# Convolution, Fourier mixer and FP8 feed-forward on one core: last stores, first loads and pixel loads moved, down's weights widened to 128 columns

## The chip, the cores and the metric

The kernel runs on one core of one Trainium2 chip. The metric is device time in microseconds of one execution; a kernel's figure is the median of several runs. A profiled execution is a run of its own, with its own time.

## What is computed

Input x has shape 64 x 55 x 55 x 96 (batch, rows, columns, channels). The first layer is a depthwise convolution with a 25 x 25 kernel of which only every third row and column is kept, and not the centre:

```python
lat = depthwise_conv(x, raw_kernel * mask, padding='SAME')
x = lat * x + bias + x
```

Then each image is a sequence of 3025 tokens of 96 channels:

```python
t = x as (64, 3025, 96)
h = relu(bn1(layernorm(t) @ w1.T))             # 192 channels
X = fft(h, over the tokens, 'ortho')
y = ifft(relu(affine(X.real, X.imag)) + 1j * relu(affine'(X.real, X.imag))).real
t = t + bn2(y @ w2.T)
t = t + ffn(layernorm(t))                      # 96 -> 384 -> 96
```

The feed-forward part rounds its operands to an 8-bit float (5 exponent, 2 mantissa bits) and its sums to a 16-bit one.

## The kernel before, in words

**Build and constants.** SyncE (SP) loads the 81 taps of each channel (`kt`) and a table of selectors (`sel`, 3.9 MB, four DMAs, line 92). ScalarE's queue loads the small parameters, and VectorE works out the constants from them. Then (lines 199 to 215) TensorE multiplies selectors with taps and so makes banded matrices, in 56 PSUM tiles `pt`; ScalarE copies the bands of the first 48 channels to `toep`, VectorE those of the other 48 to `later`, one copy each for a tile. Six DMAs (line 217) store `later` to the DRAM scratch `tb`, 8.4 MB in all.

**Convolution** (lines 222 to 327). Work goes in 12 groups: a half of the channels (48), a residue r of the row number modulo 3, a half of the batch (bh, 32 images). A group has 4 tiles of rows for r = 0 and 3 for r = 1 and r = 2, and 6 steps of 8 channels. `load` fetches the pixels `x` of one step, a tile of 384 KB by one DMA on SP, two steps ahead of use; the first two steps' loads are issued after the build. `compute` does one tile in one step: two PSUM tiles `pl` of 4 channels each, matmuls of `toep` with the pixels of the tile and its neighbours (line 253), one VectorE product (line 261) into the output buffer `buf`, one GpSimd addition of the bias (line 271). There are 8 PSUM tiles and 6 output buffers (`ob`, `NOB`). `stores` makes the list of DMAs that bring a finished buffer to the DRAM scratch `t1`: large ones of 288 KB on ScalarE's queue (line 292) and small ones of 54 or 18 KB on GpSimd's; in the last group every second large one is on SP. They are issued over the following group's steps (line 326), or at once (`early`, line 315) where the next group's tiles need the buffers; in the last group all are issued at once. During the sixth group (`halfway`) `toep` is loaded again from `tb` (line 317).

**Main stage.** After the convolution, `m1` and `m2` (0.8 and 1.0 MB) are loaded on ScalarE's queue. Each of the 64 sequences has 289 tasks on the five engines. Its `t` (121 partitions of 25 tokens, 1.16 MB) is loaded by SP (line 549; 5 buffers), VectorE takes statistics (line 560, 25 instructions), GpSimd, ScalarE and VectorE make the layer norm's factor (`variance`, `root`, `inverse`, `newton`), GpSimd scales it to `xa`, and TensorE does:

- `turn` (pa, line 587), `hidden` (ph, 609), `dft_j` (pf, 624). The result `g` (3 buffers) is put to DRAM by SP in seven puts (line 644), and fetched in another layout as `gt` (line 664);
- `dft_r` (px, line 692, the first that needs `m1` and a fetch), `project` (pd, 767 and 777), `inverse_k1` (pe, 797), back through DRAM again, `inverse_k2` (py, 859);
- the feed-forward part: `turn` (pq, 913), `up` (pu, 936), `down` (pw, 981). `down` has 75 matmuls a sequence, each with 121 token columns of the FP8 activations `hq` as weights and 96 columns of `w2q` moving. `up` has 128 columns of `w1q` as weights and up to 512 moving.

The order of all tasks is worked out when the program is built: every task has an engine, a cost and a place, and `ordered` plays the engines forward, taking tasks by place when their inputs and buffers are free. The tasks are then issued in that order, so each engine's order is fixed.

Of the kernel before, what the change touches and what calls it, by code (L numbers as in the profile page):

```python
# [50 lines left out]


@with_exitstack
def conv_attn_hybrid(ctx, tc, a, out, t1, tb, gds, eds):
# [9 lines left out]
    def const(name, shape, src=None, dt=F32, pool=None):  # L64
        x = (pool or cst).tile(shape, dt, tag=name, name=name)
        if src is not None:
            nc.scalar.dma_start(x, src)
        return x
# [4 lines left out]

    order = tc.manual_schedule()
    order.__enter__()
    with ExitStack() as cx:
        ccst = cx.enter_context(tc.tile_pool(name="c_cst", bufs=1))
        toep = ccst.tile([128, CHH, NE * TQ], F32, tag="toep", name="toep")
        cbias = ccst.tile([128, CH], F32, tag="cbias", name="cbias")
        ps = cx.enter_context(tc.tile_pool(name="c_ps", bufs=8, space=PSUM))  # L80
        xp = cx.enter_context(tc.tile_pool(name="c_x", bufs=2))
        first = cx.enter_context(ExitStack())
        selp = first.enter_context(tc.tile_pool(name="c_sel", bufs=1))
        pp = first.enter_context(tc.tile_pool(name="prep", bufs=1))
        lp = first.enter_context(tc.tile_pool(name="c_later", bufs=1))
        later = lp.tile([128, CHH, NE * TQ], F32, tag="later", name="later")
        kt = selp.tile([128, CH], F32, tag="kt", name="kt")
        nc.sync.dma_start(kt, a["taps"])
        sel = selp.tile([128, TQ, SU * TQ], F32, tag="sel", name="sel")
        for j0 in range(0, TQ, 5):  # L90
            j1 = min(j0 + 5, TQ)
            nc.sync.dma_start(sel[:, j0:j1], a["sel"][:, j0:j1])


        bns = {k: pp.tile([128, 4, w], F32, tag=f"bn{k}", name=f"bn{k}") for k, w in ((1, H), (2, CH))}
        rest = pp.tile([1, 2 * CH], F32, tag="rest", name="rest")
        vecs = [bns[1][:, :2].rearrange("p n w -> p (n w)"), bns[1][:, 2:].rearrange("p n w -> p (n w)")]
        vecs += [bns[2].rearrange("p n w -> p (n w)"), rest]
        for n, of in enumerate(vecs):
            n0, n1 = 4 * CH * n, min(4 * CH * (n + 1), 4 * (H + CH) + 2 * CH)  # L100
            nc.scalar.dma_start(of[:1], a["vec"][:, n0:n1])
        par = const("par", [128, 2, 6], a["par"])
        w1t = pp.tile([CH, H], F32, tag="w1t", name="w1t")
        nc.scalar.dma_start(w1t, a["w1t"])
        w2t = pp.tile([128, 2, CH], F32, tag="w2t", name="w2t")
        nc.scalar.dma_start(w2t, a["w2t"])
        fw1 = pp.tile([CH, FF], F32, tag="fw1", name="fw1")
        nc.scalar.dma_start(fw1, a["fw1t"])
        fw2 = pp.tile([128, 3, CH], F32, tag="fw2", name="fw2")
        nc.scalar.dma_start(fw2, a["fw2t"].rearrange("(k p) c -> p k c", p=128))  # L110
        fb1 = pp.tile([128, 3], F32, tag="fb1", name="fb1")
        nc.scalar.dma_start(fb1, a["fb1"])
        f1 = const("f1", [NJ, 4 * KHP], a["f1"])
        i2 = const("i2", [4 * KHP, NJ], a["i2"])
        ident = const("ident", [128, 128])
        ident8 = const("ident8", [NJ, NJ], dt=F8)
        w1e = const("w1e", [97, H])
        w2e = const("w2e", [128, 2, CH])
        w1q = const("w1q", [CH, FF], dt=F8)
        w2q = const("w2q", [128, 3, CH], dt=F8)  # L120
        b1q = const("b1q", [128, 3])
        b2q = const("b2q", [NJ, CH], dt=F16)
        nrd = const("nrd", [128, 2, 1])
        eps = const("eps", [NJ, 1])

        tnts = [const(f"tnt{k}", [97, 4 * NJ]) for k in range(2)]
        nc.vector.memset(eps, 1e-5)
        one = pp.tile([1, 128], F32, tag="one", name="one")
        nc.vector.memset(one, 1.0)
        ones = pp.tile([CH, CH], F32, tag="ones", name="ones")  # L130
        nc.vector.memset(ones, 1.0 / CH)
        zero = pp.tile([3 * NR1, CH], F32, tag="zero", name="zero")
        nc.vector.memset(zero, 0.0)
        for of in (toep, later):
            nc.gpsimd.memset(of[:, :, : 2 * TQ], 0.0)
            nc.gpsimd.memset(of[:, :, 16 * TQ :], 0.0)
        make_identity(nc, ident)
        for k in range(2):
            nc.gpsimd.memset(tnts[k][96:97, :], 1.0)

        for n, of in enumerate(vecs):
            width = 4 * CH if n < 3 else 2 * CH
            pv = ps.tile([128, 512], F32, tag="ps", name=f"pv_{n}")
            nc.tensor.matmul(pv[:, :width], one, of[:1], start=True, stop=True)
            if n < 3:
                nc.vector.tensor_copy(of, pv[:, :width])
        nc.vector.tensor_copy(cbias, pv[:, :CH])
        fb2q = pp.tile([NJ, CH], F8, tag="fb2q", name="fb2q")
        nc.vector.tensor_copy(fb2q, pv[:NJ, CH : 2 * CH], saturate=False)
        nc.vector.tensor_copy(b2q, fb2q)  # L150


        nc.vector.tensor_scalar(par[:, :, 4:5], par[:, :, 3:4], -1.0, None, ALU.mult)
        nc.vector.tensor_scalar(par[:, :, 5:6], par[:, :, 1:2], -1.0, None, ALU.mult)
        nc.vector.tensor_scalar(nrd, par[:, :, 0:1], -1.0, None, ALU.mult)
        bias2 = pp.tile([NR1, CH], F32, tag="bias2", name="bias2")
        for k, width in ((1, H), (2, CH)):
            bn = bns[k]
            v, r, q = (pp.tile([128, width], F32, tag=f"{x}{k}", name=f"{x}{k}") for x in ("v", "sc", "sq"))
            nc.vector.tensor_scalar(v, bn[:, 3, :], 1e-5, None, ALU.add)  # L160

            nc.scalar.activation(q, v, AF.Sqrt)
            nc.vector.reciprocal(r, q)
            nc.vector.tensor_tensor(q, r, r, ALU.mult)
            nc.vector.tensor_tensor(q, q, v, ALU.mult)
            nc.vector.tensor_scalar(q, q, -0.5, 1.5, ALU.mult, ALU.add)
            nc.vector.tensor_tensor(r, r, q, ALU.mult)
            nc.vector.tensor_tensor(r, r, bn[:, 0, :], ALU.mult)
            row, of = (w1e[96:97, :], slice(96, 97)) if k == 1 else (bias2, slice(0, NR1))
            nc.vector.tensor_tensor(row, bn[of, 2, :], r[of, :], ALU.mult)  # L170
            nc.vector.tensor_tensor(row, bn[of, 1, :], row, ALU.subtract)
            if k == 1:

                nc.vector.tensor_tensor(w1t, w1t, r[:96, :], ALU.mult)
                pm = ps.tile([128, 512], F32, tag="ps", name="pm")
                nc.tensor.matmul(pm[:CH, :H], ones, w1t, start=True, stop=True)
                nc.vector.tensor_tensor(w1e[:96, :], w1t, pm[:CH, :H], ALU.subtract)
            else:
                for h in range(2):
                    nc.vector.tensor_tensor(w2e[:, h, :], w2t[:, h, :], r, ALU.mult)  # L180

        for ed in eds:
            pad = ed.rearrange("r q k c -> q r k c")[:, :, KH, :]
            nc.sync.dma_start(pad[0], bias2)
            for q in range(1, 4):
                nc.sync.dma_start(pad[q], zero[NR1 * (q - 1) : NR1 * q])
        nc.vector.tensor_copy(w1q, fw1, saturate=False)
        nc.vector.tensor_copy(w2q, fw2, saturate=False)
        fb1q = pp.tile([128, 3], F8, tag="fb1q", name="fb1q")
        nc.vector.tensor_copy(fb1q, fb1, saturate=False)  # L190
        nc.vector.tensor_copy(b1q, fb1q)
        nc.vector.tensor_copy(ident8, ident[:NJ, :NJ], saturate=False)

        for j0 in range(0, TQ, 5):
            nj = min(5, TQ - j0)
            for e in range(2, 16):  # L200
                pt = ps.tile([128, 512], F32, tag="ps", name=f"pt_{e}_{j0}")
                for jj in range(nj):
                    for p in range(2):
                        u0 = (15 - e + 3 * p) * TQ
                        nc.tensor.matmul(
                            pt[64 * p : 64 * p + 64, jj * CH : (jj + 1) * CH],
                            sel[:, j0 + jj, u0 : u0 + 64],
                            kt,
# [807 lines left out]
    for b in range(B):  # L1016
        sequence(b)
# [127 lines left out]
```

## Time and profile before

| | us |
|---|---|
| median of 3 runs | 4634.52 (4630.35 to 4637.94) |
| the profiled execution | 4654.67 |
| its span, first to last instruction | 4652.9 |
| busy: TensorE matmuls | 4284.9 |
| busy: VectorE | 3280.7 |
| busy: ScalarE | 2963.2 |
| busy: GpSimd | 3087.5 |
| last matmul of the build ends | 61.35 |
| convolution's first matmul of the chain | 86.57 |
| convolution's last matmul ends | 950.4 |
| main stage's first matmul | 1021.7 |

A slice row divides the span into 40 equal parts; each digit is the busy share of a part in tenths. PEclk is the clock granted to TensorE, in tenths. The chain of waits goes back from the last instruction, at each step to what released it; a piece has its start, its length, and what it was. In the groups of instructions a name such as `hq` is a tile, and 128x121 is partitions by elements. PE is TensorE, PEld its weight loads, DVE VectorE, ACT ScalarE, POOL GpSimd, SP SyncE; a q after an engine is its queue. A fp32 matmul has two records.

### The profile page before, as it was taken

The numbers are of one execution on the slowest core, as the hardware profiler recorded it, in microseconds if no ns is written. First come the engines' busy times: TensorE is split into PE (matmuls) and PEld (weight loads), VectorE is DVE, ScalarE is ACT, GpSimd is POOL, SyncE is SP. The second block draws the span as 40 slices with busy tenths as digits, with TensorE's granted clock in tenths as the row PEclk, the third lists the DMA queues.
The fourth block names the chain that finished last, engine by engine and source line by source line (L and its number), as shares of the span: only waits on it lengthen the run. The fifth ranks groups of instructions, "written<-read, shape, count | busy, mean of one in ns | idle before, by whom it ended". The sixth has DMA issues, their size and how long they took to land.

```text
span 4652.9 us, 194788 instructions
## 1 busy us (share of the span) xinstructions
PE 4284.9 (92%) x83314; PEld 3569.2 (77%) x83314; DVE 3280.7 (71%) x7232; ACT 2963.2 (64%) x5947; POOL 3087.5 (66%) x4209
## 2 busy tenths in 40 slices
PE   7998798939999999999999999999999999999987
PEld 6998798937777777777777777777777777777775
DVE  4544354424888877877887788788787878788776
ACT  2000000017888888887887888888887888788875
POOL 1766576745666767766776666677766666677655
PEclk8999899969999999999999999999999999999996
DMA  4678888786666666766676666676666666667662
GB/s 162 166 193 204 245 197 207 190 185 165 165 171 178 179 177 178 181 177 169 180 183 169 169 174 179 172 185 180 176 183 169 177 174 176 171 179 183 177 162 71
DMA packets 572798, 823.14 MB, mean 177 GB/s; under 512 B 62127, under 2 KB 470276, under 8 KB 570268
## 3 DMA queue, kind: packets, MB, share of 16 engines
q1 hardware_dynamic: 442704, 736.10, 58.7%
q10 hardware_dynamic: 113036, 64.71, 7.1%
q0 software_dynamic: 16192, 9.86, 1.1%
q8 instruction: 655, 10.73, 1.0%
q14 instruction: 211, 1.73, 0.1%
HBM read 419.45 MB, written 390.64 MB: 174 GB/s over the span
## 4 chain that ended last, share of the span: by engine, by line
PE 71%; DVE 7%; DMA 7%; ACT 6%; issue 5%; POOL 2%; ACTq 2%; SPq 0%; POOLq 0%; DVEq 0%
PE pl L253 13%; PE pf L624 9%; PE ph L609 9%; PE pd L767 7%; PE px L692 7%; PE pw L981 5%; PE py L859 4%; PE pd L777 4%; PE pu L936 4%; PE pe L797 3%; PE pa L587 3%; DMA x<-in_xc_dram 2%; DMA t<-buf 2%; DVE y L945 2%; PE pq L913 2%
## 5 line engine op out<-in xcount | busy, mean ns | idle before, releaser
L253 PE MATMUL pl<-x,toep 128*64 128x96 f32 (+1 forms) x18432 | 790.1, 250 | 99.0 <-DVE buf L261 41.2
L253 PEld LDWEIGHTS pl<-x,toep 128*64 128x64 f32 (+1 forms) x18432 | 783.4, 137 | 105.7 <-issue 55.7
L945 DVE CAST y<-pu 128x1008 f16<-128x1008 f32 (+1 forms) x576 | 689.2, 1202 | 224.6 <-PE pu L936 220.5
L261 DVE SCALAR_TENSOR_TENSOR buf<-pl,x 121x384 f32<-121x384 f32 (+1 forms) x480 | 390.1, 842 | 499.0 <-PE pl L253 314.3
L609 PEld LDWEIGHTS ph<-w1e,tnt 97*121 97x121 f32 x3200 | 543.3, 185 | 210.9 <-issue 64.4
L960 ACT ACTIVATE hq<-z 128x1008 fp8e5<-128x1008 f16 (+1 forms) x576 | 601.2, 1050 | 156.7 <-DVE z L948 156.3
L718 DVE SCALAR_TENSOR_TENSOR m<-px,par,m 128x400 f32<-128x400 f32 x768 | 480.8, 626 | 286.3 <-ACT ar L709 201.6
L609 PE MATMUL ph<-w1e,tnt 97*121 97x192 f32 x3200 | 665.1, 330 | 12.9 <-ACT e L806 11.4
L271 POOL TENSOR_TENSOR buf<-buf,cbias 121x768 f32<-121x768 f32 (+1 forms) x240 | 434.1, 1821 | 363.9 <-DVE buf L261 252.1
L624 PE MATMUL pf<-h,f 121*128 121x384 f32 (+1 forms) x1664 | 664.8, 484 | 4.9 <-ACT h L618 2.6
L521 ACT ACTIVATE sm_s_a<-sm_v_a,eps 121x25 f32<-121x25 f32 x64 | 20.3, 318 | 959.0 <-POOL sm_v_a L512 956.6
L574 POOL TENSOR_TENSOR xa<-t,rstda 121x384 f32<-121x384 f32 (+1 forms) x448 | 348.2, 780 | 419.7 <-PE pa L587 411.7
L692 PE MATMUL px<-m,gt 50*64 50x50 f32 x24576 | 456.4, 220 | 63.1 <-issue 59.8
L692 PEld LDWEIGHTS px<-m,gt 50*64 50x64 f32 x24576 | 416.0, 136 | 122.0 <-issue 105.2
L725 POOL TENSOR_TENSOR sm<-ar,m 128x400 f32<-128x400 f32 x256 | 270.9, 1058 | 353.6 <-DVE m L718 296.4
L767 PE MATMUL pd<-w2e,sm 128*64 128x96 f32 x8192 | 415.7, 254 | 30.9 <-ACT g L628 18.0
L628 ACT COPY g<-pf 128x384 f32<-128x384 f32 (+1 forms) x832 | 385.6, 467 | 85.5 <-PE pf L624 70.6
L1001 POOL TENSOR_TENSOR ot<-t,o 121x480 f32<-121x480 f32 x320 | 374.3, 1177 | 91.2 <-DVE o L995 91.2
L618 ACT ACTIVATE h<-ph 121x384 f32<-121x384 f32 (+1 forms) x832 | 389.8, 488 | 68.3 <-PE ph L609 61.6
L948 DVE TENSOR_SCALAR z<-y,b1q 128x1008 f16<-128x1008 f16 (+1 forms) x576 | 418.9, 732 | 11.4
L767 PEld LDWEIGHTS pd<-w2e,sm 128*64 128x64 f32 x8192 | 358.6, 139 | 76.0 <-ACT g L628 22.5
L981 PEld LDWEIGHTS <-hq 128*121 128x121 fp8e5 x4800 | 315.9, 142 | 77.1 <-issue 37.6
(115 smaller groups left out, 8367.2 us busy)
## 6 DMA issues: line engine op xcount, KB each, us to landing
gd<-g SPq DMA_DIRECT2D x768, 192.0 KB
gt<-gd SPq DMA_DIRECT2D x512, 288.0 KB
x<-in_xc_dram SPq DMA_DIRECT2D x240, 384.0 KB
t<-t SPq DMA_DIRECT2D x64, 1050.0 KB
out_dram<-ot SPq DMA_DIRECT2D x320, 210.0 KB
t<-buf ACTq DMA_DIRECT2D x211, 288.0 KB
ed<-e SPq DMA_DIRECT2D x384, 150.0 KB
ed<-e SPq DMA_DIRECT2D x128, 131.2 KB
```

Source lines behind the costliest of these rows:

```text
L253: nc.tensor.matmul(pl[p : p + width, cc * NBS : (cc + 1) * NBS], toep[:, c0 + g + cc, o : o + width], xts[n, c0, m + d][:, g + cc, :], sta ...
L261: nc.vector.scalar_tensor_tensor(buf[:px, :, c0 + g : c0 + g + CG].rearrange("p n c -> p c n"), pl[:px, : CG * NBS].rearrange("p (c n) -> ...
L271: nc.gpsimd.tensor_tensor(part, part, cbias[:px, c1 : c1 + CC].unsqueeze(1).to_broadcast([px, NBS, CC]), ALU.add)
L609: nc.tensor.matmul(x[:NJ, q * H : (q + 1) * H], live[tnt][:, g * NJ : (g + 1) * NJ], w1e, start=True, stop=True,)
L624: nc.tensor.matmul(x[:, : nq * H], f1, live[h][:, : nq * H], start=True, stop=True)
L692: nc.tensor.matmul(x[to : to + 64].rearrange("p (q r n) -> p q r n", q=2, r=2)[:, k2p, :, o : o + NR1], y[rows, k % KC, c0 : c0 + 64], m1[ ...
L718: nc.vector.scalar_tensor_tensor(live[out_], view(px)[:, :, 256 : 256 + KC * NR1], scale, live[than], ALU.mult, ALU.max)
L767: nc.tensor.matmul(y[k % 2][64 * k2p : 64 * k2p + 64, k // 2 * CH : (k // 2 + 1) * CH], full[:, k, 64 * k2p : 64 * k2p + 64], w2e[:, 0, :] ...
L945: nc.vector.tensor_copy(live[y16][:, :n], live[pu][:, :n])
L948: nc.vector.tensor_scalar(make(z16, "z16", [128, 1024], F16)[:, :n], live[y16][:, :n], b1q[:, k : k + 1], 0.0, ALU.add, ALU.max,)
L960: nc.scalar.activation(live[hq][:, k, n0 : n0 + n], live[z16][:, :n], AF.Copy, saturate=False)
L981: nc.tensor.matmul(p[:NJ, g * CH : (g + 1) * CH], live[hq][:, k, n0 : n0 + NJ], w2q[:, k, :], start=(k == 0), stop=(k == 2),)
```

## The change

1. The pixel loads of the first two steps stand ahead of `kt` and `sel` on SP. The first two residues of each batch half change places, so that the first group has 3 tiles.
2. The other half's bands lie in three tiles, of 14, 14 and 20 channels: VectorE makes three copies for each PSUM tile, and three DMAs store them. The first two lie in a new tile `shared`.
3. Two of the six output buffers lie in `shared` as well, later four of the five `t` buffers; three others lie at the far end of the memory (`obs`) and outlive the convolution.
4. `t1` is two tensors, one for each half of the batch. Load, statistics and layer norm of sequences 0 and 1 (the first 10 tasks of each) are issued within the convolution's last two steps and behind it.
5. The last group's 36 stores are issued in the main stage, one with every third task of the order, all on SP. `m1` and `m2` are loaded on SP ahead of them.
6. `hq` has 7 more columns, zeroed once; `down` takes 128 of them as weights and writes 128 rows, of which 121 are used.
7. The zeroing of parts of `tnt`, `sm`, `sr` and `hq` is issued at their first use in the main stage. The tasks' places stand in a table (the former formulas' values, rounded to five digits). Costs and buffer counts of the planner stay.

```diff
+    def made_ahead(k):
+
+        return k // len(PLACES) < AHEAD and k % len(PLACES) < NAHEAD
+
...
+        place = k // len(PLACES) + PLACES[k % len(PLACES)]
...
+        if pool == "t":
+            if k % 5 == 4:
+                live[h] = sb("t", shape, f"t_{k}", bufs=1)
+                return live[h]
+            o = tw * (k % 5)
+            live[h] = shared[:NJ, o : o + tw].rearrange("p (h g c) -> p h g c", h=2, c=CHH)
...
-            tv = t1[b].rearrange("h (j r) c -> j h r c", r=NR1)
+            tv = t1s[b // BB][b % BB].rearrange("h (j r) c -> j h r c", r=NR1)
...
-                            p[:NJ, g * CH : (g + 1) * CH],
-                            live[hq][:, k, n0 : n0 + NJ],
+                            p[:, g * CH : (g + 1) * CH],
+                            live[hq][:, k, n0 : n0 + 128],
...
+    shared = const("shared", [128, 4 * tw])
...
-        later = lp.tile([128, CHH, NE * TQ], F32, tag="later", name="later")
+        bounds = (0, 14, 28, CHH)
+        later = [
+            shared[:, 14 * k * NE * TQ : 14 * (k + 1) * NE * TQ].rearrange("p (c n) -> p c n", n=NE * TQ)
+            for k in range(2)
+        ]
+        later.append(lp.tile([128, CHH - 28, NE * TQ], F32, tag="later2", name="later2"))
...
-        groups = [(0, r, bh) for r, bh in ((0, 0), (1, 0), (0, 1), (1, 1), (2, 0), (2, 1))]
+        groups = [(0, r, bh) for r, bh in ((1, 0), (0, 0), (1, 1), (0, 1), (2, 0), (2, 1))]
...
+        for step in steps[:2]:
+            load(*step)
+        kt = selp.tile([128, CH], F32, tag="kt", name="kt")
...
-                nc.vector.tensor_copy(later[:, :, cols], src[:, CHH:])
-        for c0 in range(0, CHH, CC):
-            nc.sync.dma_start(tb[:, c0 : c0 + CC], later[:, c0 : c0 + CC])
+                for k, of in enumerate(later):
+                    nc.vector.tensor_copy(of[:, :, cols], src[:, CHH + bounds[k] : CHH + bounds[k + 1]])
+        for k, of in enumerate(later):
+            nc.sync.dma_start(tb[:, bounds[k] : bounds[k + 1]], of)
...
-        ob = cx.enter_context(tc.tile_pool(name="c_ob", bufs=NOB))
+        ob = cx.enter_context(tc.tile_pool(name="c_ob", bufs=1))
+        obs = obx.enter_context(tc.tile_pool(name="c_obs", bufs=3, side="right"))
...
+                turn_ = (sum(NTS[r] for _, r, _ in groups[:n]) + m) % NOB
+                if turn_ < 4:
+                    pool = obs if turn_ else ob
+                    bufs_[n, m] = pool.tile([128, NBS, CHH], F32, tag="buf", name=f"buf_{n}_{m}")
+                else:
+                    o = 2 * tw * (turn_ - 4)
+                    bufs_[n, m] = shared[:, o : o + NBS * CHH].rearrange("p (n c) -> p n c", c=CHH)
...
+                if n == len(groups) - 1 and ending:
+                    for k_ in ahead[:3]:
+                        tasks[k_][3]()
+                    ahead = ahead[3:]
+                if m < early and n + 1 < len(groups):
...
+            if n == len(groups) - 1 and c0 == 3 * CC:
+                for b in range(AHEAD):
+                    tasks[len(PLACES) * b][3]()
...
-        for queue, to, of in pending:
-            queue.dma_start(to, of)
+        for k in ahead:
+            tasks[k][3]()
...
-    m1 = const("m1", [128, KHP, 2 * NR1], a["m1"], pool=late)
-    m2 = const("m2", [128, KHP, 64], a["m2"], pool=late)
+    m1 = const("m1", [128, KHP, 2 * NR1], a["m1"], pool=late, queue=nc.sync)
+    m2 = const("m2", [128, KHP, 64], a["m2"], pool=late, queue=nc.sync)
...
-        for k in ordered(bufs):
-            tasks[k][3]()
+        for n, k in enumerate(in_order):
+            if not made_ahead(k):
+                tasks[k][3]()
+            if n % 3 == 0 and pending:
+
+                to, of = pending.pop(0)[1:]
+                nc.sync.dma_start(to, of)
+                if not pending:
+                    obx.close()
```

## The prediction

> **What bounds the kernel now.** I read the page's busy times and its 40 slices first, then the busy times of chosen stretches, then the chain of waits where TensorE stands still, and last the PEld groups.
>
> ```profile
> PE   7998798939999999999999999999999999999987
> PEclk8999899969999999999999999999999999999996
> DMA  4678888786666666766676666676666666667662
> ```
>
> One slice is 116 us. TensorE is full but for the first slice, slice 9 (930 to 1047 us) and the end. The stretches (us, busy time of each engine, then clock, DMA share, GB/s):
>
> ```profile
> 16.00:62.00 46.00, 45.35 (x1065) 45.16 (x1064) 25.86 (x73) 21.73 (x57) 0.00 (x0) 1.00 0.02 5
> 66.00:82.00 16.00, 0.00 (x0) 0.00 (x0) 0.00 (x0) 0.00 (x0) 0.00 (x0) 0.51 1.02 422
> 955.00:990.00 35.00, 0.00 (x0) 0.00 (x0) 0.00 (x0) 0.00 (x0) 10.94 (x18) 0.50 0.82 159
> 990.00:1020.00 30.00, 0.00 (x0) 0.00 (x0) 7.31 (x46) 0.63 (x2) 1.55 (x7) 0.50 1.01 240
> 1500.00:4500.00 3000.00, 2870.31 (x53888) 2288.54 (x53885) 2406.76 (x5586) 2472.79 (x4960) 2099.59 (x3122) 0.99 0.68 176
> ```
>
> Two stretches have an idle TensorE and a saturated DMA: after the build (8.4 MB of the second half's table go out, pixels behind them), and from the convolution's last matmul (950.4) on. The last row is the main stage: 53,888 matmul records at 997 a sequence (83,314 less 19,506 of build and convolution, over 64) are 54.1 sequences, 55.5 us each, ScalarE busy 45.7, VectorE 44.5. The chain at the seam (start, length, what):
>
> ```profile
> 965.29 12.46 DMA t<-buf
> 977.76 12.12 DMA t<-buf
> ...
> 989.96 13.86 DMA t<-t
> ...
> 1003.90 4.10 DVE sta L560 x25
> ...
> 1009.45 10.08 issue
> ...
> 1021.70 1.85 PE pa L587 x8
> ...
> 1053.67 1.12 PE px L692 x64
> ...
> 1072.18 0.92 PE px L692 x64
> ```
>
> Last stores, first load, its statistics, then TensorE; 32 us later px, the first task that needs data written to DRAM and fetched back.
>
> **The build.** From 61.35 to 86.57 TensorE waits: 25.2 us. The pixels of two steps now stand ahead of the selectors: 6 x 0.39 = 2.36 MB, 7 us at the 339 GB/s of 5 to 10 us, so the first selectors land at some 13 us; the build starts at 15.95, behind VectorE's constants (0 to 4 us late). VectorE's copy of 240 elements (0.41 us alone, 0.34 back to back) becomes three, 0.53 us together by a fixed 0.09 us each; TensorE takes 0.82 us a group, so this hides (uncovered 56 x 0.2 = 11 us; at the end 0.2 us shows). Convolution can start at 62, but the 8.4 MB still flow until 62.2 + 19.9 (422 GB/s) + 1.5 = 83.6. By the tile sizes one of the first group's output buffers lies where the third part of the table was: VectorE waits for that part's store. TensorE runs on through 8 PSUM tiles: a step is 224 matmul records at 42.3 ns (the chain's 82.69 us for 1954) = 9.5 us, 8 tiles are step 0 and a third of step 1, 12.2 us; it stops at 74, resumes at 84.5 and ends step 1 at 91. Step 2's pixels wait for space that VectorE frees late, and land at 92. Before, those 19 us of work end at 107.5 (86.57 + 19, and 1.9 for the clock of 0.50 up to 90). Gain 15.5; without the buffer wait step 2's pixels still queue behind the table, gain 21; with late selectors and the buffer, 10. Less than nothing is excluded: the pixels now land before the build ends. I take 15.
>
> **The seam.** Two loads of t (2.3 MB) go under the last group; t1 is split by batch, so they wait only for stores long done. They stand on SP behind the last pixel load, with nothing but m1, m2 after them. Their 50 statistics (4.1 us a sequence by the row x25) go on VectorE, behind which wait the products that free PSUM tiles; VectorE is busy half of that stretch and 8 tiles are some 11 us of TensorE work, so I count 0 (5 if t comes late). The ScalarE root stands behind the sixth group's stores on ScalarE's queue, which before ended at 961. So the main stage's first matmul moves from 1021.7 to about 960. That isn't the gain: what is late next is DMA. SP now holds, in this order, m1 and m2 (1.87 MB), three loads of t (3.48 MB), and the 36 last stores (18 x 288 KB and 18 small: 6.08 MB), one at every third task, 19 of them ahead of the first put of g and all ahead of the first fetch; then the puts (2.46 MB) and one fetch (0.61 MB). With three g buffers TensorE stops after some 12 us until that put. Stores at 150 GB/s (146 from 950 to 980, 159 from 955 to 990): 40.5 us; the other 8.4 MB at 240: 35 us; landing 3: px at 951 + 78.5 = 1029.5 instead of 1053.7, a gain of 24. From there both run the same tasks (the places are the old numbers rounded to five digits, the costs unchanged, down's too). Less 4 for the convolution's end, where 2.3 MB join a DMA at 0.78 to 0.93: I take 20. Bounds: 0, and 62 if nothing waits.
>
> All on one queue: the nine stores that SP issued took 40.9 us, 4.5 each. At that price 18 large ones take SP 82 us, and with 12 for the small ones (0.66 each on GpSimd, line 315) px comes at 951 + 35 + 3 + 12 + 82 = 1083, 29 us late. Against it stands the Trainium skill, "DMA: Bandwidth & Descriptors", section "Issuing engines are not separate DMA queues": transfers from all issuers share 16 engines, and more issuers save only issue time. The trace is nearer to the rule: while SP needed 4.5 us a store, ScalarE and GpSimd ran 27 others, and the sum was 150 GB/s at share 0.8. I keep 24.
>
> The zeroing of tnt, sm, sr and hq moves into GpSimd's main stage, 0.93 + 0.76 + 0.53 us once, where it waits for puts anyway (uncovered 2.2 us). The new group order has the same tiles, stores and early counts: 0, within 5 us either way.
>
> **down with 128 columns.** The groups of weight loads (line, names, shapes, count, busy, mean ns), then pieces of the chain:
>
> ```profile
> L981 PEld LDWEIGHTS <-hq 128*121 128x121 fp8e5 x4800 | 315.9, 142 | 77.1 <-issue 37.6 <-ACT hq L960 15.2 <-ACT d L786 1.2
> L913 PEld LDWEIGHTS <-xq 121*96 121x96 fp8e5 x1600 | 124.1, 127 | 78.2 <-POOL xq L904 31.8 <-issue 16.9 <-POOL sr L725 0.5
> L936 PEld LDWEIGHTS <-w1q 96*128 96x128 fp8e5 x1152 | 102.5, 101 | 47.3 <-issue 20.3 <-DVE nc L718 2.7
> ```
>
> ```profile
> 3024.90 0.83 PE pw L981 x15
> ...
> 3031.28 1.82 PE pw L981 x30
> ...
> 3099.77 0.21 PE pq L913 x4
> ...
> 3102.82 0.43 PE pu L936 x2
> ```
>
> Down (pw) takes 55 ns a matmul. pu streams 504 columns in 215 ns, 0.43 ns each; pq's 121 columns then need 52 and take 53: bound by its columns. pw's 96 need 41 and take 55: bound by loading 121 columns of hq. The load of 128 fp8 columns (101 ns) is shorter than that of 96 (127). So with 128 columns the 96 moving ones should bind: 42 ns, 13 saved, x 75 = 0.97 us a sequence, x 64 = 62 us of TensorE work.
> Two rules of the Trainium skill ("TensorE: Matmul & The Clock Gate") bear on it. "Weight-path perf modes — Fast Weight Load (FWL) and DoubleRow" has a fast load for exactly 128 columns that aren't fp32, as the rows say. "Wait — 56ns, not 53.3ns?" speaks against: the sequencer may spend 62 ns on each matmul, and then 55 to 60 ns is its floor and the gain 0. But the px piece runs 64 records in 0.92 us, 14 ns each. I take 13 ns; more is excluded by the 96 columns. Other end: hq's columns start at odd byte offsets (121 g), w1q's don't; if that turns the fast load off, seven more columns cost 7 x 0.6 ns (the slope of 127 to 142), 4 ns, 20 us in all.
> How much of 62 shows? pw holds 6.7% of the chain from 1500 to 4500, 3.7 of its 4.15 us a sequence: at most 0.89. But TensorE's pieces add up to 50.3 of 55.5 us and ScalarE is busy 45.7; the order was set with the old cost, so part turns into waits for ScalarE and VectorE. Between 0.3 and 0.89 I take 0.6: 37 us.
>
> **Sum.** 15 + 20 + 37 = 72 us off the profiled execution (4654.67, span 4652.9): 4583. The median, 4634.52, is 20 below that execution, so 4562.5.
>
> **Rivals.**
> - The fast load stays off (15%). For: the odd offsets; no row shows such a load. Down costs 20 x 0.6 = 12: 4634.5 - 15 - 20 + 12 = 4611.5.
> - The seam gives nothing, because bytes only change places (12%). For: DMA share 0.8 to 1.0 through it. 4634.5 - 15 - 37 = 4582.5.
> - The seam gives all, puts passing between stores (12%). For: 1030 to 1050 has share 0.62. 4634.5 - 15 - 62 - 37 = 4520.5.
> - Slower (9%): SP waits for a store's landing before it can issue the next, and every put and fetch of the main stage's start stands behind that. Place: SP from 953 on. A landing takes 9.3 us (median of the nine and their like, line 315), px then starts at 1001 + 18 x 9.3 = 1168, 115 late: 4634.5 + 115 - 15 - 37 = 4697.5. It decides from 5.8 us a large store, where px is 52 late. For it: SP's longest wait there was 12 us; against it: 4.5 us a store with three issuers.
>
> **Numbers.** The sum as worked has 52%. The range, 4515 to 4620, reaches from the whole-seam case with a little more from down to the fast-load case with a poorer seam (it ends at 4631 with none). Outside it are the slow case and edges of those two. Within 0.2% (9 us, about what a measurement of this kernel can tell from no change) only the fast-load rival with a seam of nothing ends: 3%. Slower 9%, faster 88%.
>
> **What would show it.** Convolution's first matmul near 62, with a stop near 74 to 84; main stage's first matmul near 960, a TensorE gap until a put, px near 1030; PEld of hq near 100 ns and 15 pw in 0.63 us; ScalarE's share up. Wrong if PEld of hq is over 142, if px comes after 1054, or if pw's time shrinks and the period of 55.5 doesn't.

## The result, and the profile after

| | before | after |
|---|---|---|
| median of the paired runs, us | 4636.21 (4630.35 to 4637.94, 4 runs) | 4574.73 (4566.3 to 4588.28, 4 runs) |
| ratio of after to before | | 0.9872, 95% interval 0.9846 to 0.9899 |
| the profiled execution | 4654.67 | 4572.36 |
| its span | 4652.9 | 4570.5 |
| first matmul of the convolution | 85.6 | 61.1 |
| last matmul of the convolution | 950.2 | 929.6 |
| first matmul of the main stage (pa) | 1021.7 | 940.8 |
| first px | 1053.6 | 1035.2 |
| us a sequence, from 1500 to 4500 us | 55.50 | 54.63 |

The kernel is 1.28% faster, some 60 us; 72 were predicted. The period of the last row is 3000 us times 997 records a sequence, divided by TensorE's records in the stretch. One execution's milestones scatter: after and the kernel `e1_down121` below have the same code up to px, and px comes 10 us apart. A milestone of a single profile is therefore good to some 15 us.

The 40 slices of after:

```profile
PE   8999898949999999999999999999999999999996
PEclk9999999969999999999999999999999999999996
DMA  4788888876666666766666666666666666667662
```

The first slice is fuller. Slice 9 (914 to 1028 us) is almost as empty as before, 4 where it was 3. The stretches behind the build and the main stage (columns as before):

```profile
72.00:76.00 4.00, 3.47 (x84) 3.28 (x82) 0.00 (x0) 0.00 (x0) 0.00 (x0) 1.00 1.04 441
76.00:80.00 4.00, 1.91 (x48) 1.72 (x42) 0.00 (x0) 0.00 (x0) 0.00 (x0) 1.00 1.02 428
80.00:84.00 4.00, 0.00 (x0) 0.00 (x0) 0.00 (x0) 0.00 (x0) 0.00 (x0) 0.53 0.90 317
...
1500.00:4500.00 3000.00, 2853.68 (x54752) 2244.59 (x54750) 2471.53 (x5662) 2493.30 (x5011) 2120.82 (x3158) 0.99 0.68 178
```

TensorE starts the convolution at once, fills its PSUM tiles while VectorE (third busy column) does nothing, and stops from 78 to 86 us. The chain shows what it waited for, a store of the table and then VectorE's product into the output buffer that lies where this part of the table was:

```profile
64.17 20.87 DMA tb<-later
...
85.32 0.81 DVE buf L1008
...
86.18 43.87 PE pl L1000 x1006
```

In the main stage TensorE does 864 more records in 3000 us than before, with 17 us less of busy time. The group of `down`'s weight loads, and two of its pieces in the chain:

```profile
L762 PEld LDWEIGHTS <-hq 128*128 128x128 fp8e5 x4800 | 232.6, 100 | 88.4 <-issue 46.2 <-ACT hq L742 18.6 <-ACT d L572 0.5
```

```profile
3194.90 0.64 PE pw L762 x15
...
3195.97 0.72 PE pw L762 x15
```

A load takes 100 ns where it took 142, and 15 matmuls 0.64 to 0.72 us where they took 0.83. At the seam, the chain from the convolution's end to px, and then what SP issued there:

```profile
934.95 22.14 DMA t<-buf
957.11 0.87 SPq L1100
...
1018.41 0.71 SPq L1100
1019.22 2.46 SPq L432
1021.73 2.89 DMA gd<-g
...
1024.72 0.07 ACT g L416
...
1035.30 1.12 PE px L478 x64
```

```profile
958.94 27.36 SPq L1100 DMA_DIRECT2D t<-buf  x17
986.41 3.11 SPq L432 DMA_DIRECT2D gd<-g  x2
989.56 5.96 SPq L1100 DMA_DIRECT2D t<-buf  x5
995.62 3.13 SPq L432 DMA_DIRECT2D gd<-g  x2
998.85 11.07 SPq L1100 DMA_DIRECT2D t<-buf  x7
```

From 957 on the chain is almost only SP's own queue: the last stores (L1100) stand between the puts of g (L432). ScalarE can't copy into one of the three buffers g before its put has landed; it waited 49.4 us for puts in four waits, the last until 1024.6. TensorE's work behind that copy then runs up to px. This wait has taken the place of the last stores and the first load of t.

### The profile page after: what moved, and what is told of

The parts are those of the page before. It is cut to its first block, busy times and chain, and to the rows that moved or that the text cites. A ratio compares the mean times of both kernels' runs of the same rounds, so it can differ in the third digit from the quotient of the medians.

```text
span 4570.5 us, 194901 instructions
## 1 busy us (share of the span) xinstructions
PE 4227.5 (92%) x83314; PEld 3487.6 (76%) x83314; DVE 3311.5 (72%) x7344; ACT 2953.9 (65%) x5947; POOL 3071.1 (67%) x4196
## 4 chain that ended last, share of the span: by engine, by line
PE 62%; DVE 9%; DMA 9%; ACT 8%; issue 6%; POOL 4%; SPq 2%; ACTq 1%; POOLq 0%; DVEq 0%
PE pl L1000 13%; PE pf L412 9%; PE ph L397 8%; PE px L478 6%; PE pd L553 6%; PE py L644 4%; PE pu L718 3%; PE pd L563 3%; PE pe L583 3%; PE pa L376 2%; DMA x<-in_xc_dram 2%; PE pw L762 2%; DVE y L727 2%; POOL xq L686 1%; ACT m L495 1%
## 5 line engine op out<-in xcount | busy, mean ns | idle before, releaser
L363 POOL TENSOR_TENSOR xa<-shared,rstda 121x384 f32<-121x384 f32 (+1 forms) x364 | 283.2, 781 | 366.7 <-PE pa L376 360.8
L1008 DVE SCALAR_TENSOR_TENSOR buf<-pl,x 121x384 f32<-121x384 f32 (+1 forms) x336 | 270.9, 842 | 291.8 <-PE pl L1000 176.9
L1018 POOL TENSOR_TENSOR buf<-buf,cbias 121x768 f32<-121x768 f32 (+1 forms) x168 | 303.4, 1819 | 237.2 <-DVE buf L1008 184.9
L412 PEld LDWEIGHTS pf<-h,f 121*128 121x128 f32 x1664 | 293.3, 192 | 93.0 <-ACT h L406 24.0
L782 POOL TENSOR_TENSOR ot<-shared,o 121x480 f32<-121x480 f32 x260 | 304.3, 1178 | 81.2 <-DVE o L776 81.2
```

The source lines that it names most:

```text
L412: nc.tensor.matmul(x[:, : nq * H], f1, live[h][:, : nq * H], start=True, stop=True)
L782: nc.gpsimd.tensor_tensor(halves(y), live[t][:, :, 5 * q : 5 * q + 5], halves(live[o16]), ALU.add)
```

## The experiments

Twelve kernels, each timed against the kernel before on its chip. The median of the kernel before differs from one comparison to the next (4625 to 4643 us), so kernels are compared by their ratios. The lead at 900 us is the surplus of TensorE's records over the kernel before, at the convolution's 23.6 records a us; the lead at px is 1053.6 less the time of the first px. Both are from one execution each.

| kernel | ratio | 95% interval | lead at 900 | lead at px |
|---|---|---|---|---|
| after | 0.9872 | 0.9846 to 0.9899 | 18.6 | 18.4 |
| e1_down121 | 0.9933 | 0.9907 to 0.9959 | 26.0 | 29.0 |
| e2_down128_alone | 1.0020 | 1.0002 to 1.0039 | 0.4 | 3.0 |
| t_fixed_ring | 1.0006 | 0.9983 to 1.0028 | -1.1 | 6.1 |
| x_places_and_down | 0.9866 | 0.9842 to 0.9889 | 2.1 | 23.7 |
| e5_pixels_behind_build | 0.9923 | 0.9896 to 0.9951 | 10.4 | 10.6 |
| e4_seam_undone | 0.9847 | 0.9822 to 0.9871 | 28.1 | 46.9 |
| e7_one_t1 | 0.9867 | 0.9839 to 0.9895 | 21.7 | 42.0 |
| e9_seam_undone_down121 | 0.9903 | 0.9878 to 0.9928 | 25.9 | 46.3 |
| e3_own_queues | 0.9820 | 0.9793 to 0.9847 | 23.4 | 52.7 |
| e6_stores_after_fetch | 0.9895 | 0.9866 to 0.9923 | 18.9 | 76.0 |
| q_stores_scalar_gpsimd | 0.9837 | 0.9811 to 0.9864 | 18.8 | 43.1 |
| c_own_queues_down_cost | 1.0592 | 1.0565 to 1.0618 | 25.8 | 50.2 |

A difference of two ratios has an interval of some 0.0037 to either side (the two half-widths, added as squares and the root taken), 17 us.

**e1_down121**: after, with `down` as before.

```diff
-                            p[:, g * CH : (g + 1) * CH],
-                            live[hq][:, k, n0 : n0 + 128],
+                            p[:NJ, g * CH : (g + 1) * CH],
+                            live[hq][:, k, n0 : n0 + NJ],
```

> The kernel after with down's weights back at 121 columns (all else as after). My theory: the wider weights are worth more than the 37 us of the prediction, because the main stage's period fell from 55.5 to 54.6 us a sequence, 53 us in all; the medians leave 43 for it beside 18 at the first px. So this kernel comes out 40 to 62 us over the kernel after (4575), at 4615 to 4637, its period back at 55.5 us and the PEld of hq back near 142 ns. Rival: the shorter period is from the other parts (t buffers at fixed places, layer norms made ahead); then it stays within 15 us of 4575.

Measured 4604.0 us, ratio 0.9933: 0.0061 above after, 28 us give or take 17, and less than the 40 to 62 that were expected. The weight load is back at 138 ns. So within the changed kernel `down` is worth some 0.4 of the 68 us of TensorE time that it saves, and by the interval 0.2 to 0.7.

**e2_down128_alone**: before, with only `down` changed (`hq` in a fixed tile with seven zeroed columns more).

```diff
+    hqp = late.tile([128, 3, NJ * NR1 + 7], F8, tag="hq0", name="hq0")
+    padded["hq"] = [hqp]
...
-                            live[hq][:, k, n0 : n0 + NJ],
+                            live[hq][:, k, n0 : n0 + 128],
```

> The kernel before with 128 weight columns in down alone. If the wider weights work by themselves, this is 40 to 60 us under the kernel before (4636), at 4576 to 4596, with the PEld of hq near 100 ns and conv and seam as before (first px near 1054). If they need the rest of the change, less than 25 us.

Measured 4652.88 us, ratio 1.0020 with an interval of 1.0002 to 1.0039: 9 us lost, give or take 9. The weight load takes 99 ns here too, so the saving is there, and no time comes of it:

```profile
1500.00:4500.00 3000.00, 2830.30 (x53483) 2227.37 (x53482) 2422.39 (x5578) 2461.39 (x4940) 2092.16 (x3117) 0.99 0.69 176
```

TensorE was busy 40 us less than before in these 3000 us, and did 405 records fewer: it waited more. This miss led to x and t.

**e5_pixels_behind_build**: after, with the first pixel loads behind the table's stores again.

```diff
-        for step in steps[:2]:
-            load(*step)
...
             nc.sync.dma_start(tb[:, bounds[k] : bounds[k + 1]], of)
         first.close()
+        for step in steps[:2]:
+            load(*step)
```

> The kernel after with the first pixel loads behind the table's stores, as before. The prediction had 15 us for this step, the trace has the convolution's end 24 us earlier: 4590 to 4599. First matmul of the convolution near 86 again. If the convolution's later stalls absorb the early start, within 6 us of the kernel after.

Measured 4608.81 us, ratio 0.9923: 24 us above after, give or take 18. The convolution starts at 85.5 us again. At 150 us its lead, counted in the same way, is -0.4 us, where the nine kernels with pixels ahead have 9.6 to 15.6, 12.7 in the mean; at 900 us it is 10.4, where they have 18.6 to 28.1, 23.0 in the mean. Both put the pixels at some 13 us.

**e4_seam_undone**: after, with no task made ahead, the last stores issued at once on their three queues, and `m1`, `m2` on ScalarE's. t and its buffers keep their new places.

```diff
-AHEAD, NAHEAD = 2, 10
+AHEAD, NAHEAD = 0, 10
...
-                if m < early and n + 1 < len(groups):
+                if m < early:
...
         order.__exit__(None, None, None)
+    obx.close()
```

> The kernel after with the seam as before: no task made ahead, last stores issued at once on three queues, m1 and m2 on ScalarE's queue. My theory now: the seam's part of the change gave nothing (from the convolution's last matmul to the first px it is 109 us after and 103 before), so this is within 10 us of the kernel after, with first px at 1025 to 1040. The prediction's 20 us would make it 4595; a gain hidden elsewhere in the trace would too.

Measured 4568.89 us, ratio 0.9847: 0.0025 below after, which the intervals don't part from zero. px came 89 us after the convolution's last matmul, in after 106, before 103. So the spreading itself gained nothing. Undoing it did not undo the seam, though: the loads of t still moved forward, for SP issued them from 917 us on, ahead of the last stores. They go to `shared`, where no buffer of the last group lies, and wait only for the stores of the group ahead of it.

**e7_one_t1**: e4, with t1 one tensor as before.

```diff
-            t1s = [dp.tile([BB, 2, NTOK, CHH], F32, tag=f"t1_{k}", name=f"t1_{k}") for k in range(BH)]
+            t1 = dp.tile([B, 2, NTOK, CHH], F32, tag="t1", name="t1")
+            t1s = [t1[BB * k : BB * (k + 1)] for k in range(BH)]
```

> The kernel with the seam undone (tasks not made ahead, stores at once) and t1 one tensor again, as in before. From the convolution's last matmul to the first px the seam-undone kernel took 90 us and before 103; if that comes of the split (sequence 0's load no longer waits for the last stores), this one is back at 101 to 105, and 12 us slower than the seam-undone kernel (ratio near 0.987). If dependencies are kept by region anyway, within 5 us of it (ratio 0.9847).

Measured 4559.37 us, ratio 0.9867, and px 83 us behind the convolution's end: with the seam undone the split of t1 gives nothing that shows.

**e9_seam_undone_down121**: e4 with e1's edit.

> The kernel with the seam undone and down back at 121 columns. Down's wider weights gave 28 us (e1 against after) in the kernel after and nothing (9 us slower) in the kernel before. If they pay in every kernel with the other parts, this one is 25 to 40 us over the seam-undone kernel, ratio 0.990 to 0.993. If what they pay depends on the seam (tasks ahead, stores spread), the difference is under 10 us, ratio under 0.987.

Measured 4579.75 us, ratio 0.9903: 0.0056 above e4, 26 us give or take 16, and 0.0036 above e7. That repeats e1. It also says that the rest of the change (places, group order, pixels, and the small parts with them), without `down` and without the spreading, is worth 45 us.

**x_places_and_down**: e4 with the pixels behind the build and the old group order; of the change the places of the buffers and tiles, the three-part table, the split of t1 and `down` are left.

> The seam-undone kernel with the first pixels behind the build and the groups in the old order: what is left of the change is where the tiles lie (two output buffers and four t buffers in one fixed tile), t1 in two tensors, and down with 128 columns. Down alone in before cost 9 us (period 55.9 us a sequence, TensorE's idle for issue 2.1 us); in kernels with the other parts it gave 17 to 28 (periods 54.6 to 55.3, issue 1.4 to 1.7). Theory A: it is the places of tiles that let down pay, and that bring the loads of t forward at the seam; then the ratio is 0.988 to 0.992, period near 55.0, issue near 1.5, first px at 1020 to 1035. Theory B: down pays only where convolution and seam ran differently; then period near 55.9 and ratio over 0.993. The convolution's length (85 to its last matmul, 865 us before, 848 with the new group order and the pixels behind the build) tells where its 17 us came from: 848 here, the buffers' places; 865, the group order.

Measured 4561.35 us, ratio 0.9866: as fast as after. So this part of the change is enough for the whole gain. What the rest adds doesn't show in the total: x and after differ by 0.0006, give or take 0.0035.

**t_fixed_ring**: e2, with the five t buffers in one fixed tile.

```diff
+    ring = late.tile([NJ, 5 * tw], F32, tag="ring", name="ring")
...
+        if pool == "t":
+            o = tw * (k % 5)
+            live[h] = ring[:, o : o + tw].rearrange("p (h g c) -> p h g c", h=2, c=CHH)
```

> The kernel before with down at 128 weight columns and the five t buffers in one fixed tile (a ring of five slots that lies where the convolution's tiles do not); pixels, group order, output buffers and the seam's code as before. Theory A (a fixed place of t is what lets down pay): 54.6 to 55.1 us a sequence in the main stage against 55.9 for down alone, TensorE idle on ScalarE 1.4 to 1.5 us a sequence against 2.1, first pixel matmul at 1030 to 1050, and a ratio of 0.986 to 0.994. Theory B (it is another of the places or pools that the change moves, the output buffers or the order in which pools are opened): 55.7 to 56.1 us a sequence, and a ratio of 1.000 to 1.004, as for down alone.

Measured 4626.8 us, ratio 1.0006, 55.26 us a sequence: no gain, as for `down` alone. My expectation misdescribed the ring. `late` opens behind the convolution, so the ring lies in memory that the convolution's tiles held, and its loads waited for the last stores all the same. SP in t, then in x:

```profile
942.31 41.86 SPq L315 DMA_DIRECT2D t<-buf  x9
992.03 15.97 SPq L559 DMA_DIRECT2D ring<-t  x10
```

```profile
926.56 26.71 SPq L339 DMA_DIRECT2D shared<-t  x8
958.40 30.38 SPq L1065 DMA_DIRECT2D t<-buf  x9
```

In x the loads stand ahead of the stores, and px comes at 1029.9 instead of 1047.5. A fixed tile is not enough; it must lie where nothing of the last group lies.

**e3_own_queues**: after, with each spread store on the queue that its list names (ScalarE and SP in turn, small ones on GpSimd) instead of all on SP.

```diff
-                to, of = pending.pop(0)[1:]
-                nc.sync.dma_start(to, of)
+                queue, to, of = pending.pop(0)
+                queue.dma_start(to, of)
```

> The kernel after with the 36 late stores each on the queue that its list names (large ones on ScalarE's and SP's in turn, small ones on GpSimd's), still one with every third task. In the trace of after the stores move 115 GB/s on average from 965 to 1020 at a DMA share of 0.70, all on SP's queue, against 150 at 0.80 on three queues before. Theory A (one queue moves 576-byte rows more slowly than three): the first px moves from 1035 to 1015 to 1022, the ratio to before falls by 0.003 to 0.004. Theory B (only the bytes and their place ahead of the puts count): px within 6 us of 1035. Theory C: ScalarE now stands in its queue's back-pressure and px comes later.

Measured 4542.23 us, ratio 0.9820: 0.0052 below after, 24 us give or take 17, and the lowest ratio of all, though e4 and q are within the intervals. px comes at 1000.9, 78 us behind the convolution's end. The stretches of the seam, of after and then of e3:

```profile
960.00:990.00 30.00, 8.55 (x34) 6.30 (x34) 6.71 (x42) 5.80 (x15) 5.81 (x18) 0.67 0.75 133
990.00:1020.00 30.00, 13.99 (x40) 10.90 (x41) 0.00 (x0) 6.64 (x17) 2.48 (x3) 0.61 0.70 125
```

```profile
960.00:990.00 30.00, 17.05 (x58) 12.85 (x57) 1.06 (x6) 9.86 (x25) 10.66 (x24) 0.72 0.80 165
990.00:1020.00 30.00, 29.45 (x535) 23.75 (x536) 11.01 (x21) 23.53 (x51) 15.33 (x24) 0.94 0.78 190
```

The last two columns are DMA share and GB/s. The same stores, spread over the same tasks, are under way from 960 to 990 at 165 instead of 133 GB/s, with other transfers among them. In e3 the last one is issued at 984, in after at 1018; from 990 on e3's TensorE is busy for 29.45 of 30 us.

**q_stores_scalar_gpsimd**: e3, with all large last stores on ScalarE's queue.

```diff
-                    nc.sync if last and i % 2 else nc.scalar,
+                    nc.scalar,
```

> The kernel with the late stores on their own queues, but no large one on SP: all 18 on ScalarE's queue, small ones on GpSimd's, so that SP holds only loads, puts and fetches. If puts were late for the stores ahead of them on SP, the first px comes at 980 to 995 (1001 with half of the large ones on SP) and the total is 0 to 15 us lower (ratio 0.979 to 0.982). If ScalarE, whose copies stand behind 18 stores that its queue takes only slowly, becomes the bound, px comes later than 1001 and the ratio is over 0.982.

Measured 4550.57 us, ratio 0.9837, px at 1010.5: not better than e3, nor parted from it by the intervals. Clearing SP of stores altogether gains nothing more.

**e6_stores_after_fetch**: after, with no store before the 170th task.

```diff
-            if n % 3 == 0 and pending:
+            if n >= 170 and n % 3 == 0 and pending:
```

> The kernel after with the late stores starting at task 170 of the order, behind the first sequence's seven puts and its first two fetches. If the stores' place ahead of the puts is what makes px late, px comes at 985 to 1000, and the total falls by 10 to 30 us against after, unless the second sequence's puts stand behind the stores instead and give it back. If the bytes are the bound anyway, the total stays within 8 us of after.

Measured 4580.31 us, ratio 0.9895. px came at 977.6, the earliest of all, and gained nothing:

```profile
1020.00:1050.00 30.00, 0.00 (x0) 0.00 (x0) 0.00 (x0) 0.00 (x0) 0.00 (x0) 0.50 0.70 113
```

For these 30 us every engine stands still, while SP issues 18 of the stores that were put off, with puts of g between them, and the DMA moves 113 GB/s. The wait is moved behind px and comes back whole.

**c_own_queues_down_cost**: e3, with the planner's cost of `down` at 0.70 instead of 0.84.

> The kernel with the late stores on their own queues, and the planner told that down now costs 0.70 us for its 15 matmuls (0.84 before; the trace has 0.70 to 0.73). Of 1.0 us a sequence that TensorE saves, 0.4 show in the period. If the order that was set for the old cost keeps the rest from showing, the period falls by another 0.2 to 0.4 us and the total by 13 to 26 us under the same kernel with the old cost (ratio 0.976 to 0.979). If ScalarE and VectorE take it, no order helps: within 5 us (0.981 to 0.983), or worse.

Measured 4895.47 us, ratio 1.0592. Another order came out, with 61.2 us a sequence, TensorE waiting 3.4 us a sequence for nothing that the profile shows (1.4 in e3). The clock granted to TensorE from 1500 to 4500 us was 0.96, in e3 0.99. The planner's costs steer an order; a truer cost of one task made a much worse one.

## Why the prediction was right or wrong, step by step

The sum was 72 us and came out at 60. The mechanism of the build and of `down` was right, and the sizes were near; the seam's 20 us were lost whole. At px after leads by 18 us and e1, with the same code up to there, by 29, and `down` gave 28, give or take 17: together 46 to 57 of the 60. That the total came so near is in part luck, for the convolution gained more than the build's 15, from terms that were put at zero.

**Build: 15, measured some 13** (e5, at 150 and at 900 us; the medians of e5 and after differ by 24, give or take 18). The mechanism held: the chain above has the store of the table, VectorE's product into the buffer, and then TensorE. The stop was foreseen from 74 to 84.5 us and came from 78 to 86: TensorE did some 400 records first, where 8 tiles are 299 (12.6 us, not 12.2), for VectorE still finished some products before it stopped at 72.

**New group order: 0, and some 7 us by 900 us.** From 150 to 900 us the ten kernels with the new order gain 5.1 to 16.5 us on the kernel before, 10.4 in the mean and 10.8 in e5. x, with the old order and the new places, gains 3.6 in its one execution; e2 and t, with the old convolution, 1.9 and -0.5. So the ranges don't meet, but the size is loose. I counted tiles, stores and early counts, not which buffer is waited for at a change of group.

**Seam: 20, measured 0.** This is the step that failed. The forecast of px, 1030, looks right beside 1035, but only because the convolution ended 21 us earlier. From the convolution's last matmul to px the time should have fallen from 103 to some 79; it was 106. Two terms of the sum were too small.

- The stores, 40.5 us at 150 GB/s. The term took the speed of a stretch in which three issuers shared the stores, and used it for one. A large and a small store took SP 3.1 us together (29 stores in the 44.39 us of the three rows above) where 150 GB/s would have been 2.3, and the puts stood between and behind them. From 959, where the run of stores begins, px took 76 us; for what was left then the sum has some 61 (40.5, 17.6 for 4.2 MB at 240 GB/s, and 3). In e1 and e5 it took 77 and 76.
- The time ahead of them. For `m1`, `m2` and two loads of t, 4.2 MB, the sum has 17 us. SP came to the run of stores 29 us behind the convolution's end (24 in e1, 34 in e5), for it waited on stores of the convolution that had not landed; one of them took 22.14 us in the chain above. The sum put no such wait.

Two numbers were on the table: the row, 4.5 us a large store on SP, and the rule of the Trainium skill ("DMA: Bandwidth & Descriptors", "Issuing engines are not separate DMA queues"). By the rule px comes 79 us behind the convolution's end, by the row at 132. Measured 106, between them. The 4.5 us were not a price of issuing: in before SP spent 39.6 us in eight waits for landings around those nine stores. With three queues (e3) px comes 78 us behind, the sum's figure, but by other rates (276 GB/s from 934 to 960 us, 165 from 960 to 990). In this case the issuers were thus worth 28 us to px, and 24 or 32 when e1 or e5 stands for after. Whether SP's own processing or the waiting of puts behind stores in one queue weighs more is not parted by these runs; e6 shows that the two together can hold all engines.

The rival "the seam gives nothing" was right about the amount and wrong about the reason. It wasn't bytes that only change places: e3 moves the same bytes and gains. The slow rival, SP waiting for each landing, is out in after: SP issued 17 stores, large and small, in 27.36 us, 1.6 each. The rival "the seam gives all" is out as well: puts did pass between stores, and px came no nearer to the convolution's end.

**Places of t and the output buffers: 0, measured 14 to 20 at the seam.** The prediction reckoned with places only in the build, where one delays VectorE; that loads of t could start early it put down to the split of `t1`, and in e7 they do so without it. With the seam undone, e4, e7, e9 and x reach px 83 to 89 us behind the convolution's end where before took 103, and in all of them SP issues the loads of t ahead of the last stores. t_fixed_ring, where the loads stay behind them, has px at 103 behind it. In after itself this gain is what the single queue took back.

**down: 37, measured 28 give or take 17.** The TensorE term was right: 4.94 us a sequence became 3.88, 14.1 ns a matmul where 13 were predicted. So the 62 ns a matmul that the same skill gives the sequencer with hardware decode off ("TensorE: Matmul & The Clock Gate", "Wait — 56ns, not 53.3ns?") don't bind here. (The 14 ns of px in the prediction are those of a record; a fp32 matmul has two, and so takes 29 ns, which is still less.) Odd byte offsets don't turn the fast load off either: in after the loads that start at odd ones, every second, took 99.9 ns in the mean, the others 99.8. The rival of 15% is out. The factor 0.6 can't be told from the measured 28 of 68 us, 0.4, within its interval.

Where the rest goes is partly seen. VectorE's addition behind `down` became slower, five times a sequence: the two rows below are of before and of after, from 1500 to 4500 us (count, busy time, mean ns).

```profile
L995 DVE TENSOR_TENSOR o<-o,b2q 121x480 f16<-121x480 f16 x270 | 175.3, 654 | 117.4 <-ACT o L990 73.9 <-POOL sm L725 43.5
```

```profile
L776 DVE TENSOR_TENSOR o<-o,b2q 121x480 f16<-121x480 f16 x273 | 211.3, 780 | 96.7 <-ACT o L771 49.2 <-POOL sm L511 45.3 <-ACT g L416 0.3
```

The operation, its shape and its type are the same; it costs 0.6 us a sequence more, where TensorE saves 1.06. The traces' records show what is behind it. Where no GpSimd instruction is running at its start, the addition takes at most 410 ns. Where one is, it takes the rest of that instruction and some 265 ns more. Before has 213 of the second kind among 320 (788 ns in the mean), after 243 (889 ns). An addition of the second kind ends a fixed time behind GpSimd, however early it starts, and so can swallow what `down` saved ahead of it. That it does so isn't shown: e2, t and x have nearly the same counts (236, 239 and 241), and gain differently. Every engine's order is also still the one that the old cost made.

What I did not foresee is that the factor depends on the rest of the kernel. Alone it is 0 (e2: 9 us lost, give or take 9; t: 3 lost, give or take 10). With the new places and the same order x is 65 us faster than t, give or take 15, of which 18 are at px. The other 47 lie behind it and **stay open**: TensorE's instructions stand in the same order in both, and so do ScalarE's main tasks. The clock can account for some 10 us at most: from 1100 to 4500 us TensorE was granted half of it for 82 us in t and for 61 in x. What differs is where tiles lie, when they come free, and that four tiles are zeroed at their first use. Which of these lets `down` pay was not tried one by one.

## What to carry to other kernels

A milestone that comes when predicted proves little unless the one before it does too: subtract them. When transfers are moved to one queue, use the rate of one queue from the trace, not of a stretch where several shared the work, and look at what stands behind them in that queue. Where a buffer lies in memory can decide when its first load may start, and this was worth more here than the order in which loads and stores were written down. What a faster task pays can depend on the rest of the kernel: here 28 us in one and nothing in another, with the same task made equally faster.

## What the runs showed of the hardware that was not expected

- FP8 weight loads of 128 columns took 100 ns on average, at odd and at even byte offsets alike (99.9 and 99.8 ns in after), as those of `w1q` (101 ns before); 121 columns took 142.
- VectorE's fp16 addition of 121x480 took 654 to 658 ns on average in the three kernels with 121 columns, 777 to 792 in the ten with 128 columns and the same order of tasks, and 618 in `c_own_queues_down_cost`, with 128 columns and another order. So it isn't the columns as such but what GpSimd does at that moment. In all fourteen traces the addition took at most 410 ns when no GpSimd instruction was running at its start; when one was, it took the rest of that one and then 261 to 279 ns (the middle 80% of the cases).
- While SP alone issued the last stores of after (957 to 1019 us), the DMA moved 127 GB/s at a share of 0.70. While three queues issued most of those of e3 (945 to 984), it moved 206 GB/s at 0.89. Other transfers are among them in both.
